# Five small changes to the start, the joint and the end of an attention and convolution kernel

## The chip, the cores and the metric

One NeuronCore of one Trainium2 chip. The metric is the device time of one execution in microseconds (us), the median of several. Lower is better.

## The reference

Sixteen images of 128 channels and 32 x 32 pixels pass an attention block, then a block of two quantized 3x3 convolutions.

```
# attention: 4 heads, 1024 tokens of 128 channels
qkv    = einsum('bchw,oc->bohw', x, w_qkv) + b_qkv
attn   = softmax(q @ k * c**-0.5)
x      = einsum('bchw,oc->bohw', attn @ v, w_out) + b_out + x
# convolutions: activations to 4 bits, weights to 4 bits; batch normalization with the statistics
# of the whole batch (16 x 32 x 32 values of each channel)
out = batchnorm(conv3x3(act_quant(x),   weight_quant(w1)), gamma1, beta1)
out = batchnorm(conv3x3(act_quant(out), weight_quant(w2)), gamma2, beta2)
return out + x
```

The batch statistics are what matters: no value of the second convolution's input is known before the last matmul of the first convolution, and no output before the last matmul of the second.

## The kernel before

`wvo_sb` holds the value and output weights; they are multiplied into one matrix on TensorE (`fold_b`, tile `ps_b`) before any value can be projected. The start (cut):

```python
nc.sync.dma_start(out=wqk_sb[0 : P // 2, 0], in_=wqk[0 : P // 2, 0])
nc.scalar.dma_start(out=wqk_sb[P // 2 :, 0], in_=wqk[P // 2 :, 0])
nc.sync.dma_start(out=xt[0][:, ts(0, HALF)], in_=x[0][:, ts(0, HALF)])
nc.scalar.dma_start(out=xt[0][:, ts(1, HALF)], in_=x[0][:, ts(1, HALF)])
nc.scalar.dma_start(out=wvo_sb, in_=wvo)
nc.sync.dma_start(out=wqk_sb[:, 1:], in_=wqk[:, 1:])
load(1)
# ...
warm_up(3)
fold_a(0)
for hf in range(NHF):
    project_u(0, hf)
fold_b()
# ... then, step by step: scores(g, j), project_v, attend one step later
```

The attention body in the middle (some 2030 us) is untouched. One piece of convolution, with its copy out of PSUM (the memory that the matmuls of this kernel write to) and, for the last image alone, its statistics straight from PSUM:

```python
def conv(pool, tag, b, n, r, rows=RPH, group=None):
    ps = pool.tile([P, rows, W], F32, tag=tag, name=f"psc{n}_{b}_{r}")
    for tap in range(NTAP):
        ...                                     # nine matmuls, bf16
    ps = ps.rearrange("p h w -> p (h w)")
    nc.scalar.copy(ys[b][:, r * W : (r + rows) * W], ps)
    if group is not None:
        nc.vector.bn_stats(place(n, b, group), ps)
    return last
```

The tiles for the statistics stand in memory just ahead of the output tiles:

```python
early = [keep.tile([P, (B - LATE) * NHF, STATS], F32, name=f"early{n}") for n in range(2)]
late = [
    keep.tile([P, 3 + (LATE * NHF + 1 - n) * STATS], F32, name=f"late{n}") for n in range(2)
]
# ...
ys = [keep.tile([P, N], F32, name=f"y{b}") for b in range(B)]
```

Between the convolutions `keep_clock` issues 21 matmuls whose result nobody reads, so that TensorE does not stand idle. Then the second convolution and the output (B is 16 images, H 32 rows, RPH 16 rows, NHF 2 halves of an image, N 1024 values of a row of a tile):

```python
for r0, r1 in ((0, RPH + 1), (RPH + 1, H)):       # 17 and 15 rows of 32
    quantize(0, ys[0], scale1, bias1, r0, r1)      # ScalarE, then two steps on VectorE
quantize(1, ys[1], scale1, bias1)
for b in range(B):
    for hf in range(NHF):
        conv(ps_c, "c", b, 1, hf * RPH, group=hf if b == B - 1 else None)
    ...
scale2, bias2 = bn_params(1)
for b in range(B):
    parts = NHF if b == 0 else 1
    for i in range(parts):
        cut = ts(i, N // parts)
        y = ys[b][:, cut]
        nc.scalar.activation(y, y, AF.Identity, bias=bias2, scale=scale2)
        nc.vector.tensor_tensor(y, y, x1[b][:, cut], ALU.add)
        nc.sync.dma_start(out=out[b][:, cut], in_=y)
```

## Time and profile before

| | us |
|---|---|
| time, median of 3 runs | 2154.43 (2154.38 to 2155.27) |
| time of the one execution that was profiled | 2156.01 |
| its span | 2154.1 |
| TensorE busy | 2118.2 (98%) |
| first matmul that needs the value weights | 10.13 |
| end of the last matmul of convolution 1, start of the first of convolution 2 | 2054.18, 2059.34 |
| end of the last matmul of convolution 2, end of the bias of its normalization | 2122.99, 2126.33 |

The chain of work that ended last is read from its end backwards: each line is a stretch of time and what the next line waited for. A line of DMA, of ACT (ScalarE) or of DVE (VectorE) in it, between lines of PE (TensorE), is time in which TensorE had nothing that it could start, or filled with matmuls that nobody reads. The prediction shows the lines of the start and of both joints.

The page's view by stretches shows the stores. Its columns are: the stretch, its length, busy us and number of instructions of PE, PEld, DVE, ACT and POOL, the granted TensorE clock, the share of the DMA engines, and GB/s. The kernel before, while the first stores go out:

```profile
2129.00:2130.00 1.00, 0.00 (x0) 0.00 (x0) 0.96 (x1) 1.00 (x2) 0.00 (x0) 0.50 0.99 383
2130.00:2131.00 1.00, 0.00 (x0) 0.00 (x0) 1.00 (x2) 1.00 (x2) 0.00 (x0) 0.50 0.15 55
2131.00:2132.00 1.00, 0.00 (x0) 0.00 (x0) 1.00 (x2) 1.00 (x2) 0.00 (x0) 0.50 0.92 381
```

Image 0 goes out by 2130, then the DMA stands still for most of a microsecond until image 1 is ready; from there on it is never idle.

### The profile page before, as it was taken

To read this page: it belongs to the slowest core of one execution; us is meant where nothing else is said; L and a number is where in the kernel's file an instruction comes from. 1 tells how busy PE (TensorE), PEld (TensorE's weight loads), DVE (VectorE), ACT (ScalarE), POOL (GpSimd) and SP (SyncE) were. 2 spreads that over 40 slices of the span, in tenths; PEclk is the share of its full clock that TensorE was granted. 3 is DMA by queue.
4 is the path that set the end of the run, shared out by engine and by line. 5 is a ranking of instruction groups with operands and counts; after the bars stand their busy time and mean duration, and the time that the engine had idled before them with its cause. 6 is when DMAs were issued, how large, how long until landed. Compare 5 with 4: busy or idle time off the path is not lost.

```text
span 2154.1 us, 14436 instructions
## 1 busy us (share of the span) xinstructions
PE 2118.2 (98%) x5293; PEld 947.3 (44%) x5294; DVE 1256.5 (58%) x1791; ACT 695.3 (32%) x764; POOL 6.8 (0%) x16
## 2 busy tenths in 40 slices
PE   9999999999999999999999999999999999999994
PEld 4444444444444444444444444444444444444541
DVE  3665565556456565556646555665655655665676
ACT  2233232333233333333323323333332333323355
POOL 0000000000000000000000000000000000000000
PEclk9999999999999999999999999999999999999997
DMA  1000000000000000000000000000000000000043
GB/s 60 11 20 0 0 20 0 20 0 10 10 0 20 0 20 0 0 20 0 20 0 20 0 0 20 0 20 0 18 3 0 20 0 10 1 0 10 0 166 157
DMA packets 10606, 36.79 MB, mean 17 GB/s; under 512 B 1440, under 2 KB 1568, under 8 KB 10528
## 3 DMA queue, kind: packets, MB, share of 16 engines
q1 hardware_dynamic: 9872, 33.76, 4.2%
q10 hardware_dynamic: 656, 2.03, 0.3%
q8 instruction: 43, 0.70, 0.1%
q14 instruction: 35, 0.29, 0.0%
HBM read 19.01 MB, written 16.78 MB: 17 GB/s over the span
## 4 chain that ended last, share of the span: by engine, by line
PE 98%; DVE 1%; DMA 0%; ACT 0%; issue 0%; ACTq 0%; DVEq 0%
PE pss L480 41%; PE psa L504 40%; PE psc L275 6%; PE psv L459 5%; PE psu L448 5%; PE psa L619 1%; DVE y L777 1%; DMA wvo_sb<-in_wvo_dram 0%; ACT y L776 0%; DVE late L285 0%; PE ps_b L420 0%; ACT y L283 0%; DVEq L963 0%; PE ps_a L412 0%; ACTq L386 0%
## 5 line engine op out<-in xcount | busy, mean ns | idle before, releaser
L480 PE MATMUL pss<-u,x 128*128 128x512 f32 (+1 forms) x2064 | 962.4, 589 | 0.0
L504 PE MATMUL psa<-e,vo 128*128 128x512 f32 x2016 | 947.6, 592 | 0.0
L493 ACT ACTIVATE e<-pss 128x1024 f32<-128x1024 f32 x511 | 522.9, 1023 | 1305.3 <-PE pss L480 1269.2
L515 DVE TENSOR_TENSOR es<-es,e 128x1024 f32<-128x1024 f32 x378 | 461.3, 1220 | 475.3 <-ACT e L493 471.5
L480 PEld LDWEIGHTS pss<-u,x 128*128 128x128 f32 x2064 | 392.1, 190 | 487.2 <-issue 467.8
L504 PEld LDWEIGHTS psa<-e,vo 128*128 128x128 f32 x2016 | 382.6, 190 | 471.4 <-issue 466.4
L467 DVE COPY vo<-psv 128x512 f32<-128x512 f32 x128 | 88.2, 689 | 259.7 <-PE psv L459 259.7
L275 PE MATMUL psc<-pad,wq 128*128 128x512 bf16 (+3 forms) x585 | 132.0, 380 | 0.6 <-DVE pad L250 0.6
L448 PE MATMUL psu<-x,at_sb 128*128 128x512 f32 x256 | 131.1, 594 | 0.2 <-DVE at_sb L414 0.2
L459 PE MATMUL psv<-bt_sb,x 128*128 128x512 f32 x256 | 130.4, 592 | 0.0
L453 DVE TENSOR_SCALAR u<-psu,au_sb 128x512 f32<-128x512 f32 x64 | 47.9, 749 | 87.2 <-PE psu L448 87.2
L275 PEld LDWEIGHTS <-wq 128*128 128x128 bf16 x585 | 56.7, 97 | 79.9 <-issue 15.3
L527 DVE TRANSPOSE_TENSOR_REDUCE part<-es 128x32 f32<-128x1024 f32 (+1 forms) x66 | 80.6, 1221 | 2.2
L562 DVE STREAM_TRANSPOSE rb<-sums 128x1024 f32<-128x1024 f32 (+1 forms) x66 | 80.1, 1213 | 2.3
L513 DVE TENSOR_TENSOR es<-e,e 128x1024 f32<-128x1024 f32 x63 | 76.6, 1216 | 0.0
L448 PEld LDWEIGHTS psu<-x,at_sb 128*128 128x128 f32 x256 | 48.8, 191 | 61.3 <-issue 60.5
L459 PEld LDWEIGHTS psv<-bt_sb,x 128*128 128x128 f32 x256 | 48.6, 190 | 61.2 <-issue 61.2
L573 DVE TENSOR_TENSOR av<-av,rb 128x1024 f32<-128x1024 f32 x47 | 57.6, 1226 | 3.3
L574 DVE TENSOR_TENSOR acc<-acc,av 128x1024 f32<-128x1024 f32 x47 | 57.4, 1221 | 1.0
L283 ACT COPY y<-psc 128x512 f32<-128x512 f32 (+2 forms) x65 | 37.5, 578 | 59.2 <-PE psc L275 58.7
L520 ACT COPY av<-psa 128x512 f32<-128x512 f32 x63 | 36.9, 586 | 44.6 <-PE psa L504 44.6
L553 DVE COPY side<-part 32x32 f32<-32x32 f32 x252 | 43.0, 171 | 4.7
(98 smaller groups left out, 467.2 us busy)
## 6 DMA issues: line engine op xcount, KB each, us to landing
x_dram<-x SPq DMA_DIRECT2D x16, 512.0 KB, 2.6
res<-x_dram SPq DMA_DIRECT2D x16, 512.0 KB, 9.9
x<-in_x_dram SPq DMA_DIRECT2D x15, 512.0 KB, 3.6
out_dram<-y SPq DMA_DIRECT2D x15, 512.0 KB, 4.7
raw<-in_cw_dram ACTq DMA_DIRECT2D x2, 576.0 KB, 3.7
wvo_sb<-in_wvo_dram ACTq DMA_DIRECT2D x1, 514.0 KB, 7.8
out_dram<-y SPq DMA_DIRECT2D x2, 256.0 KB, 2.0
wqk_sb<-in_wqk_dram SPq DMA_DIRECT2D x1, 385.5 KB, 7.0
```

Of the source, the lines that this page charges most:

```text
L275: last = nc.tensor.matmul(ps, lhsT=wq[n][:, tap, :], rhs=pads[b % NPAD][:, r + dy : r + dy + rows, dx : dx + W], start=(tap == 0), stop=(t ...
L448: nc.tensor.matmul(ps, lhsT=at_sb[:, h, :], rhs=xt[b][:, ts(hf, HALF)], start=True, stop=True)
L459: nc.tensor.matmul(ps, lhsT=xt[b][:, ts(j, P)], rhs=bt_sb.rearrange("p h o -> p (h o)"), start=True, stop=True,)
L467: nc.vector.tensor_copy(vos[b, j], ps)
L480: last = nc.tensor.matmul(ps[:, ts(m, N // len(parts))], lhsT=xt[b][:, ts(key, P)], rhs=us[g][:, queries], start=True, stop=True,)
L493: exps[:] = [nc.scalar.activation(e, ps, AF.Exp).ins]
L504: nc.tensor.matmul(psa[g][m], lhsT=vos[b, j][:, ts(h, P)], rhs=e[:, ts(m, HALF)], start=(j == 0), stop=(j == NCH - 1),)
L513: nc.vector.tensor_tensor(es[g], es.pop((g, 0)), es.pop((g, 1)), ALU.add)
L515: added = nc.vector.tensor_tensor(es[g], es[g], es.pop((g, j)), ALU.add)
L527: nc.vector.tensor_reduce(part, total.rearrange("p (k c) -> p k c", c=Q), AX.X, ALU.add, apply_transpose=True,)
L562: nc.vector.transpose(rb, rinv.unsqueeze(2).to_broadcast([P, n, Q]))
L573: nc.vector.tensor_tensor(av, av, rb, ALU.mult)
```

## The change

Its intent: let the value weights land earlier, take the copy out of the chain ahead of the statistics, begin and end the second convolution with pieces of 8 rows so that the quantization ahead of it and the statistics behind it are short, and begin storing earlier.

```diff
@@ -227,7 +227,7 @@
     STATS = nc.vector.BN_STATS_DIM
     early = [keep.tile([P, (B - LATE) * NHF, STATS], F32, name=f"early{n}") for n in range(2)]
     late = [
-        keep.tile([P, 3 + (LATE * NHF + 1 - n) * STATS], F32, name=f"late{n}") for n in range(2)
+        keep.tile([P, 3 + (LATE * NHF + 1) * STATS], F32, name=f"late{n}") for n in range(2)
     ]
     for n in range(2):
         nc.gpsimd.memset(late[n][:, 0:1], float((B - LATE) * N))
@@ -280,9 +280,9 @@
                 stop=(tap == NTAP - 1),
             )
         ps = ps.rearrange("p h w -> p (h w)")
-        nc.scalar.copy(ys[b][:, r * W : (r + rows) * W], ps)
         if group is not None:
             nc.vector.bn_stats(place(n, b, group), ps)
+        nc.scalar.copy(ys[b][:, r * W : (r + rows) * W], ps)
         return last
 
     def statistics(b, n):
@@ -384,7 +384,8 @@
         nc.scalar.dma_start(out=wqk_sb[P // 2 :, 0], in_=wqk[P // 2 :, 0])
         nc.sync.dma_start(out=xt[0][:, ts(0, HALF)], in_=x[0][:, ts(0, HALF)])
         nc.scalar.dma_start(out=xt[0][:, ts(1, HALF)], in_=x[0][:, ts(1, HALF)])
-        nc.scalar.dma_start(out=wvo_sb, in_=wvo)
+        nc.sync.dma_start(out=wvo_sb[0 : P // 2], in_=wvo[0 : P // 2])
+        nc.scalar.dma_start(out=wvo_sb[P // 2 :], in_=wvo[P // 2 :])
         nc.sync.dma_start(out=wqk_sb[:, 1:], in_=wqk[:, 1:])
         load(1)
         nc.sync.dma_start(out=bo_sb, in_=bo)
@@ -666,7 +667,7 @@
             ps = ps_a.tile([P, HALF], F32, tag="a0", name="unread")
             flat = wq[0].rearrange("p t o -> p (t o)")
             with tc.issue_after(convs[0]):
-                for _ in range(21):
+                for _ in range(16):
                     nc.tensor.matmul(
                         ps, lhsT=wq[1][:, 0, :], rhs=flat[:, 0:HALF], start=True, stop=True
                     )
@@ -751,12 +752,15 @@
             t = resp.tile([P, N], F32, name=f"res{b}")
             nc.sync.dma_start(out=t, in_=x1d[b])
             x1.append(t)
-        for r0, r1 in ((0, RPH + 1), (RPH + 1, H)):
+
+        for r0, r1 in ((0, 10), (10, RPH + 2), (RPH + 2, H)):
             quantize(0, ys[0], scale1, bias1, r0, r1)
         quantize(1, ys[1], scale1, bias1)
+        starts = {0: (0, 8, RPH, H), B - 1: (0, RPH, H - 8, H)}
         for b in range(B):
-            for hf in range(NHF):
-                conv(ps_c, "c", b, 1, hf * RPH, group=hf if b == B - 1 else None)
+            rows = starts.get(b, (0, RPH, H))
+            for i, (r0, r1) in enumerate(zip(rows, rows[1:])):
+                conv(ps_c, "c", b, 1, r0, r1 - r0, group=i if b == B - 1 else None)
             if b + 2 < B:
                 quantize(b + 2, ys[b + 2], scale1, bias1)
             if b < B - 1:
@@ -769,13 +773,15 @@
         scale2, bias2 = bn_params(1)
 
         for b in range(B):
-            parts = NHF if b == 0 else 1
-            for i in range(parts):
-                cut = ts(i, N // parts)
-                y = ys[b][:, cut]
-                nc.scalar.activation(y, y, AF.Identity, bias=bias2, scale=scale2)
-                nc.vector.tensor_tensor(y, y, x1[b][:, cut], ALU.add)
-                nc.sync.dma_start(out=out[b][:, cut], in_=y)
+            ends = (0, N // 4, N // 2, N) if b == 0 else (0, N)
+            for lo, hi in zip(ends, ends[1:]):
+                y = ys[b][:, lo:hi]
+                if (b, lo) == (0, 0):
+                    nc.vector.tensor_scalar(y, y, scale2, bias2, ALU.mult, ALU.add)
+                else:
+                    nc.scalar.activation(y, y, AF.Identity, bias=bias2, scale=scale2)
+                nc.vector.tensor_tensor(y, y, x1[b][:, lo:hi], ALU.add)
+                nc.sync.dma_start(out=out[b][:, lo:hi], in_=y)
     outer.close()
 
 
```

## The prediction

> **What bounds the kernel now.** I read the page's busy times first, then the chain of work that ended last over the whole span, then the same chain and the order of time at the start (0 to 30 us) and at the end (2028 us on), and last the stretches of the DMA.
>
> From the page: TensorE is the bound nearly everywhere.
>
> ```profile
> PE 2118.2 (98%) x5293; PEld 947.3 (44%) x5294; DVE 1256.5 (58%) x1791; ACT 695.3 (32%) x764; POOL 6.8 (0%) x16
> ```
>
> 98% of 2154.1 us leaves 36 us in which TensorE does not work. Nothing in the change touches the attention body, so all that can be won lies in those 36 us: the start, the joint between the two convolutions, and the output. Chain of work at the start (start us, length us, what):
>
> ```profile
> 2.22 7.77 DMA wvo_sb<-in_wvo_dram
> 9.99 0.14 issue
> 10.13 1.13 PE ps_b L420 x8
> ```
>
> The value weights land at 9.99, TensorE waits for them (its own wait there is 2.85 us, 7.28 to 10.13), and everything after is continuous on TensorE; so an earlier landing moves all the rest. The chain at the end:
>
> ```profile
> 2048.07 6.11 PE psc L275 x36
> 2054.18 0.02 issue
> 2054.20 0.41 ACT y L283
> 2054.61 0.02 issue
> 2054.63 0.48 DVE late L285
> ...
> 2057.21 0.85 ACT qt L248
> 2058.06 0.02 issue
> 2058.08 0.45 DVE qt L249
> 2058.53 0.02 issue
> 2058.56 0.73 DVE pad L250
> 2059.29 0.05 issue
> 2059.34 63.66 PE psc L275 x288
> 2122.99 0.02 issue
> 2123.02 0.59 ACT y L283
> 2123.61 0.02 issue
> 2123.63 0.71 DVE late L285
> ...
> 2126.36 3.79 ACT y L776 x4
> ```
>
> So each convolution ends in copy, then statistics, then eight tiny instructions, and only then do quantization and the next convolution (or the output) begin. After 2126.36 the output pass is limited by the stores: in the stretches after it the DMA moves 86, 383 and 55 GB/s in the three microseconds from 2128, then 381 and from 2132 on about 410 GB/s until 2150. There is a hole at 2130 to 2131, and after it the stores never run dry.
>
> [...] the statistics, which only read the same PSUM tile as the copy, start 0.02 us after the copy ends. [...] The trace has 0.724 us for 544 columns written as 17 rows, 0.430 for 512 as 16 rows, 0.658 for 480 as 15 rows[...] In the trace the idle 2.85 us at the start cost nothing (granted clock 1.00), so the shorter holes after the change should not either.
>
> **The change part by part**, in us against the time before.
>
> A. Value weights. Ahead of wvo or beside it now go wqk of head 0 (0.13 MB), x of image 0 (0.52 MB), wqk of the other heads (0.39 MB) and, alternating, part of x of image 1. The DMA packets of wvo start at 5.73, most engines are through at 7.8, one straggling engine ends at 9.38, and 0.6 later it counts as landed. After the change half of wvo goes where wqk of the other heads went, the other half runs beside those. About 0.4 to 0.6 MB less moves before wvo is complete; at the 330 to 410 GB/s of these stretches that is 1.0 to 1.8. The landing should come at 8.2 to 9.0, still after the 7.28 at which TensorE becomes free, so all of it counts. **-1.5.** The other heads' wqk came at 8.97 and is first read at 16.25; 1 to 2 us later does no harm.
>
> B. Statistics ahead of the copy, end of convolution 1. The statistics (0.48) start after the matmuls instead of after the 0.41 copy: -0.43. But the copy (0.40) now sits in ScalarE's queue ahead of the square root, which is ready 0.02 + 0.30 after the statistics: +0.05. And the order of instructions on VectorE moves around 2045: the statistics of the piece of 480 columns (0.63) and a quantization step (0.27, which itself waits for ScalarE until about 2045.55) now stand ahead of the transposing reduction of the last softmax sums. In the trace before:
>
> ```profile
> 2044.99 0.70 DVE L527 TRANSPOSE_TENSOR_REDUCE part<-es 128x16 f32<-128x512 f32 x1
> 2045.62 0.63 DVE L285 BATCH_NORM_STATS2 late<-psc 128x6 f32<-128x480 f32 x1
> 2046.16 0.51 PE L545 MATMUL psr<-part,quad 128*128 128x8 f32 x4
> ```
>
> The reduction ended at 2045.69, TensorE read it at 2046.16. Worked anew: statistics 2044.99 to 2045.62, step to 2045.82, reduction 2045.75 to 2046.45, so TensorE's psr can start at 2046.50, 0.34 later, with everything behind it: +0.34. Sum of B: **-0.04**; the gain is nearly lost.
>
> C. Quantization before convolution 2, from bias to first matmul. Was 0.85 + 0.45 + 0.73 (544 columns, 17 rows). For 10 rows: ScalarE 0.85 less 224 columns at 0.83 ns = 0.66; first VectorE step between 0.28 (256) and 0.44 (544): 0.31; second step[...] between 0.30 (256) and 0.43 (512): 0.33. 1.30 against 2.03: **-0.73**. Do the later chunks come in time? From the bias: the second chunk is padded at about 2.0, wanted at 2.45; the third, which waits for one of two buffers, at 3.0, wanted at 3.5; image 1 at 4.8, wanted at 5.4. Thin, but enough. The 16 filler matmuls (0.22 each, 3.5) end inside the hole of now 4.0; 21 of them (4.6) would have blocked the convolution, so their cut belongs to the gain.
>
> D. Splits at both ends of convolution 2. 18 matmuls more, at half width. The last 18 pieces of convolution 1, of 256 and 288 columns, took 0.12 each (6.11 less 18 x 0.22, over 18), against 0.22 for 512: two halves cost about 0.003 to 0.006 more each. **+0.10.**
>
> E. End of convolution 2. Copy 0.59 and two issue steps gone, statistics of 256 columns (0.43, as the 256-column piece of convolution 1) for 512 (0.71): -0.90; the copy ahead of the square root +0.05, a slightly longer aggregation +0.02. **-0.83.**
>
> F. First stores. The first store is issued about 0.8 after the bias instead of 1.6. But the hole in the DMA before image 1 stays, because that store waits for ScalarE's 1024 columns and VectorE's addition. ScalarE did 512, 512, 1024 before image 1 was ready; now 256 goes to VectorE and it does 256, 512, 1024. One 256-column step of ScalarE is 0.21. The stores of images 1 to 15 then run at 410 GB/s as before. **-0.21**, not -0.8.
>
> Sum: -1.5 - 0.04 - 0.73 + 0.10 - 0.83 - 0.21 = -3.2, so 2154.43 - 3.2 = 2151.2 us.
>
> **Rivals.** R1: wvo is limited by the straggling engine, not by its place in the queue. For it: one engine ended 1.6 after most others. Then A is -0.8 and the time 2151.9. If, on the contrary, the landing falls to 7.3, A is -2.8 (TensorE's own work until 7.28 stops it there) and the time 2149.9. R2: the VectorE reordering does not stall TensorE (the reduction has some slack that I put too low), or stalls it more: 2150.9 or 2151.6. R3: a wait takes the place of the shortened quantization: the third chunk or image 1 comes late and TensorE stands at 2062; for it, thin slack of 0.4 to 0.6; against it, VectorE's writes with even rows are faster. It would give back up to 0.7: 2151.9. R4: the earlier first store is worth its full 0.8, if the store engines' total were the limit from the first byte; against it the hole in the DMA at 2130. Then 2150.6. R5: with fewer filler matmuls the clock falls for convolution 2. Against it the 2.85 us hole at the start with a granted clock of 1.00. [...]
>
> **Range and chances.** The terms' errors (A 0.5, B 0.3, C to F 0.3 together) and about 0.5 of spread between runs (the three runs span 0.9) make some 0.9 as one standard deviation at most, so 2149.6 to 2152.9. The whole change is 0.15% of the time; 2% would be 43 us, more than all of TensorE's idle time. So within 2% is all but certain.
>
> **What would show it.** A: wvo lands at 8.2 to 9.0 and TensorE's ps_b follows at once. B: the statistics wait for TensorE, not ScalarE; a stall of 0.3 to 0.4 ahead of psr, with the reduction as the releaser. C: 1.4 to 1.5 from bias to first matmul, one hole of about 0.5 behind the filler matmuls. D: the convolution takes 63.75 from first to last matmul. E: some 2.5 from last matmul to bias, against 3.34. F: a hole in the DMA still ahead of image 1's store. The prediction is wrong if TensorE waits inside convolution 2, if the clock falls below 1.00 there, or if wvo lands as late as before.

## The result

| | before | changed |
|---|---|---|
| time, median of 6 runs, us | 2154.41 (2154.34 to 2155.27) | 2153.41 (2152.61 to 2155.77) |
| span of the profiled execution | 2154.1 | 2151.1 |
| its time | 2156.01 | 2153.01 |

The ratio is 0.9995, with a 95% interval of 0.9982 to 1.0008. A ratio here is the mean time of one kernel's fast runs over that of the other's of the same rounds, so not quite the ratio of the medians. The predicted range was 2149.6 to 2152.9; the median lies 0.5 us above it.

The two profiles differ by 3.0 us, nearly the 3.2 that was predicted, and the medians by 1.0. The prediction was right about one pair of executions, by luck as the runs below show (a late landing before, an ordinary one after), and wrong about the kernels. The page of the changed kernel:

```profile
PE 2117.1 (98%) x5306; PEld 948.0 (44%) x5307; DVE 1256.9 (58%) x1796; ACT 696.1 (32%) x767; POOL 6.9 (0%) x16
```

Its chain at the start:

```profile
2.22 6.61 DMA wvo_sb<-in_wvo_dram
...
8.92 1.13 PE ps_b L421 x8
```

And at the joint and the end (L284 is now the statistics, L285 the copy):

```profile
2053.26 0.48 DVE late L284
...
2053.76 0.35 ACT y L285
...
2054.16 0.40 ACT rt L314
...
2055.84 0.66 ACT qt L248
...
2056.52 0.34 DVE qt L249
...
2056.88 0.34 DVE pad L250
...
2057.27 63.70 PE psc L275 x306
...
2120.99 0.44 DVE late L284
...
2123.48 4.71 ACT y L782 x5
```

The copy has left its place ahead of the statistics and stands, as predicted, ahead of the square root `rt`. From the end of the last matmul (2053.23) to the first of convolution 2 (2057.27) the joint is now 4.04 us instead of 5.16. The stall in front of `psr` is there too (`psr` are the matmuls that read `part`, the softmax sums that VectorE has just reduced). In the order of time (start us, length us, instruction, and in brackets the idle time before it and what ended it):

```profile
2043.58 0.66 DVE L284 BATCH_NORM_STATS2 late<-psc 128x6 f32<-128x480 f32 x1
...
2044.35 0.71 DVE L528 TRANSPOSE_TENSOR_REDUCE part<-es 128x16 f32<-128x512 f32 x1
...
2045.11 0.52 PEld L546 LDWEIGHTS psr<-part,quad 128*128 128x128 f32 x4 [0.39 <-DVE part L528]
```

The reduction now follows the statistics, and TensorE stands for 0.39 us until it is done.

### The profile page after: what moved, and what is told of

It reads as the page before. It is cut to its first block, busy times and chain, and to the rows that moved or that the text cites. A ratio compares the mean times of both kernels' runs of the same rounds, so it can differ in the third digit from the quotient of the medians.

```text
span 2151.1 us, 14475 instructions
## 1 busy us (share of the span) xinstructions
PE 2117.1 (98%) x5306; PEld 948.0 (44%) x5307; DVE 1256.9 (58%) x1796; ACT 696.1 (32%) x767; POOL 6.9 (0%) x16
## 4 chain that ended last, share of the span: by engine, by line
PE 98%; DVE 1%; ACT 0%; DMA 0%; issue 0%; ACTq 0%; DVEq 0%
PE pss L481 41%; PE psa L505 40%; PE psc L275 6%; PE psv L460 5%; PE psu L449 5%; PE psa L620 1%; DVE y L783 1%; DMA wvo_sb<-in_wvo_dram 0%; ACT y L782 0%; PE ps_b L421 0%; DVEq L969 0%; PE psr L546 0%; DVE late L284 0%; PE ps_a L413 0%; ACTq L386 0%
## 5 line engine op out<-in xcount | busy, mean ns | idle before, releaser
L285 ACT COPY y<-psc 128x512 f32<-128x512 f32 (+3 forms) x67 | 37.9, 565 | 59.1 <-PE psc L275 53.8
```

## The experiments

Since most of TensorE's work is a fixed chain, two executions can be compared by a few marks. The first four columns of this table are read from the traces (us); the last is the time, the median of five runs (one run where marked), with that of the kernel before of the same call in brackets. "Body" is from the start of `ps_b` to the start of the last matmul of convolution 1, "conv 2" from its first matmul to its end, "end" from there to the first store packet of image 1, "stores" from that packet to the end of the last one.

| run | ps_b starts | body | end | stores | time (before) |
|---|---|---|---|---|---|
| before, first profile | 10.13 | 2043.75 | 8.15 | 20.42 | |
| changed, first profile | 8.92 | 2044.01 | 7.09 | 20.95 | |
| b_again | 8.68 | 2043.75 | 8.15 | 20.22 | 2154.70 (2155.43) |
| a_only | 8.81 | 2043.75 | 8.15 | 20.60 | 2154.57 (2155.43) |
| no_a | 9.02 | 2044.21 | 7.07 | 20.93 | 2153.35 (2155.43) |
| no_stall | 8.36 | 2043.75 | 7.08 | 20.96 | 2152.24 (2155.43) |
| b_shift | 9.99 | 2043.75 | 8.15 | 20.64 | 2155.28 (2155.12) |
| align | 9.41 | 2043.75 | 7.08 | 20.30 | 2152.48 (2155.12) |
| late_b | 8.34 | 2043.12 | 7.08 | 20.69 | 2151.39 (2155.12) |
| a_again | 8.62 | 2044.11 | 7.08 | 20.98 | 2153.39 (2155.12) |
| b_again2 | 9.10 | 2043.75 | 8.15 | 20.36 | 2154.97 (2154.67) |
| a_only2 | 9.46 | 2043.76 | 8.15 | 20.55 | 2154.79 (2154.67) |
| b_shift64 | 8.98 | 2043.75 | 8.14 | 20.62 | 2154.95, one run (2154.67) |
| b_shift128 | 9.15 | 2043.75 | 8.14 | 20.65 | 2155.15, one run (2154.67) |

Convolution 2 took 63.64 us in every run with its old pieces and 63.69 in every run with the new ones. All runs gave the correct result. The kernel before, in three calls of nine runs, had medians of 2155.43, 2155.12 and 2154.67, and single runs from 2154.13 to 2157.25: a difference of half a microsecond between two medians of five proves nothing, and where it matters the marks decide. The experiments ran on three chips. Of all these ratios only that of no_stall has an interval that leaves out 1 (0.9984, 0.9970 to 0.9998), and all are within 2%.

### b_again: the kernel before, unchanged

> The kernel before, unchanged, to see how one execution differs from another. Theory 1 (the profile that the prediction read was of a slow execution: its time was 2156.0 against a median of 2154.4, and the excess sits in the start): the value weights land at about 8.4 instead of 9.99, TensorE's ps_b starts at about 8.5, the span is about 2152.5, and time minus span stays 1.9. Theory 2 (the start was typical, the excess sits in the output): wvo lands at 9.9 to 10.1 again and the stretch from the last bias (2126.3) to the end of the span is 26 us instead of 27.8. Theory 3 (noise of the chip's clock): the stretch from ps_b to the end of convolution 1, 2044.05 us on TensorE, is longer or shorter by 1 us or more. Time against before: same, within 0.3 us, in all three.

The profiled execution took 2154.22 us. Chain at the start:

```profile
2.22 6.33 DMA wvo_sb<-in_wvo_dram
...
8.68 1.13 PE ps_b L420 x8
```

The same kernel starts `ps_b` 1.45 us earlier than in its first profile, by the landing alone. The body is equal to 0.01 us, so is everything up to the stores, and the time less the span is 1.9. That is theory 1, for 1.45 of the 1.79 us between the two executions; the rest lies behind the first store of image 1. The first profile shows a late landing: its last packet of `wvo` ended at 9.38, here at 8.04. In time the expectation (within 0.3 us of before) failed: 2154.70 against 2155.43, for one and the same kernel.

### a_only: the split of the value weights alone, on the kernel before

```diff
-        nc.scalar.dma_start(out=wvo_sb, in_=wvo)
+        nc.sync.dma_start(out=wvo_sb[0 : P // 2], in_=wvo[0 : P // 2])
+        nc.scalar.dma_start(out=wvo_sb[P // 2 :], in_=wvo[P // 2 :])
```

> Only the split of the value weights. Theory 1: the landing is within 0.5 of that of the kernel before of the same call (8.3 to 8.9), and the time within 0.5 us of before. Theory 2: the landing is 1.1 to 1.5 earlier than that of before, and so is the time: -1.2 us.

2154.57 us against 2154.70 for b_again. That is 0.86 below the kernel before of the call, more than the 0.5 of theory 1, but b_again, which is that kernel, was 0.73 below it too. `ps_b` is not earlier (8.81 against 8.68). Theory 2 falls.

### no_a: the changed kernel without that split

> The changed kernel with the value weights loaded by one transfer, as before. Theory 1: as fast as the changed kernel, -1.0 to -1.6 us against before, since the other parts are worth 1.7 us by the two profiles. Theory 2: the other parts give less than that in the unprofiled runs; the time is within 0.5 us of before.

2153.35 us, against 2153.41 and 2153.39 of the changed kernel: what the change gains, it gains without its first part. The median is 2.1 below the kernel before of this call, more than expected; but that kernel's median was high here by 0.7 (it is the same kernel as b_again).

### no_stall: the old order for one piece

```diff
+        copy_first = (n, r) == (0, 0)
+        if copy_first:
+            nc.scalar.copy(ys[b][:, r * W : (r + rows) * W], ps)
         if group is not None:
             nc.vector.bn_stats(place(n, b, group), ps)
-        nc.scalar.copy(ys[b][:, r * W : (r + rows) * W], ps)
+        if not copy_first:
+            nc.scalar.copy(ys[b][:, r * W : (r + rows) * W], ps)
```

> The changed kernel, but the copy of the first piece (480 columns) of the last image of convolution 1 stays ahead of its statistics, so that VectorE's order there is that of before. Both theories: no idle time of TensorE ahead of psr (0.39 us in the changed kernel's profile), TensorE's chain from ps_b to the last matmul of convolution 1 is 0.25 to 0.4 us shorter than 2044.31, and the time 0.3 us below the changed kernel's.

```profile
2043.01 0.70 DVE L532 TRANSPOSE_TENSOR_REDUCE part<-es 128x16 f32<-128x512 f32 x1
...
2043.63 0.63 DVE L287 BATCH_NORM_STATS2 late<-psc 128x6 f32<-128x480 f32 x1
2044.18 0.63 PEld L550 LDWEIGHTS psr<-part,quad 128*128 128x128 f32 x4
```

The reduction is first again, and TensorE does not wait. The body is 2043.75 as before the change; in the changed kernel it was 2044.01, 2044.11 and (no_a) 2044.21. So the stall costs 0.26 to 0.46 us, and it comes from the order of two instructions on VectorE. The time fell by 1.1 us, more than the stall accounts for (0.3 was expected). In the profiled run the rest is the start, which was early (`ps_b` at 8.36); in the other four no trace shows it. None of the five was 2 us above the others, as one of six and two of five of the changed kernel's were.

### b_shift, b_shift64, b_shift128: where the output tiles start

In every run of the changed kernel the stores took some 20.95 us, and in the kernel before 20.2 to 20.6. The prediction had taken them as equal. In the trace the single store packets (4096 bytes, one row of a tile) were longer, 163.6 ns in the mean against 159.7. The diff has one line that nobody would take for a change in speed: `late1` grew from 27 to 33 values, for the added statistics. In the built programs it takes 32 bytes more for that, and all sixteen tiles `y` behind it start 32 bytes past a multiple of 256 instead of on one: `y0` stands at byte 32256 of each partition before, at 32288 in the changed kernel and in b_shift, at 32512 in align. So I moved them in the kernel before, with whatever stands behind them, and changed nothing else:

```diff
+    keep.tile([P, 8], F32, name="shift")     # 32 bytes; 16 and 32 values in the other two
     ys = [keep.tile([P, N], F32, name=f"y{b}") for b in range(B)]
```

> The kernel before with an unused tile of 32 bytes ahead of the output tiles y, so that each row of them starts 32 bytes past a multiple of 256, as in the changed kernel; nothing else. Theory (the store packets are slower from such addresses): mean packet time of the 1920 stores of images 1 to 15 goes from 159.7 ns to 163.6, the stretch from their first to their last packet from 20.2-20.6 us to 20.9, the time +0.4 to +0.5 us. Rival (the slower stores come from the 256-column first stores, or from VectorE's new work beside them): packets stay at 159.7 ns and the time at that of before.

> The kernel before with 64 unused bytes ahead of y, so rows start 64 bytes past a multiple of 256. If any start off a multiple of 256 costs the same, the mean store packet takes 163 to 164 ns; if a start on a multiple of 64 is enough, 159.7 ns.

> The same with 128 bytes. 163 to 164 ns if only multiples of 256 are fast, 159.7 ns if multiples of 64 or 128 are enough.

Mean length of the 1920 packets that store images 1 to 15, computed from the packets in each trace:

| tiles y start at | runs | ns |
|---|---|---|
| a multiple of 256 bytes | before, b_again, b_again2, a_only, a_only2, align, late_b | 159.6 to 159.8 |
| 32 past it | changed, a_again, no_a, no_stall, b_shift | 163.5 to 163.6 |
| 64 past it | b_shift64 | 163.9 |
| 128 past it | b_shift128 | 164.2 |

The same in the stretches, 16 us in the midst of the stores; first the kernel before, then b_shift:

```profile
2132.00:2148.00 16.00, 0.00 (x0) 0.00 (x0) 14.16 (x13) 12.85 (x12) 0.00 (x0) 0.50 1.02 415
```

```profile
2132.00:2148.00 16.00, 0.00 (x0) 0.00 (x0) 14.03 (x13) 12.73 (x12) 0.00 (x0) 0.50 1.02 405
```

The engines are fully busy in both (share 1.02) and move 2.4% less in b_shift. The changed kernel itself:

```profile
2129.00:2145.00 16.00, 0.00 (x0) 0.00 (x0) 14.06 (x13) 12.76 (x12) 0.00 (x0) 0.50 1.02 406
```

So each of the three starts off 256 costs, by 2.4 to 2.8% a packet; by what mechanism, no run here shows.

While all 16 engines are at work the cost stands clear of any spread: from the first packet of image 1 until the number of packets in flight falls below 12 for good, counted in each trace, takes 18.83 to 18.91 us in the seven aligned runs and 19.42 to 19.46 in the other seven. In the last 1.2 to 1.9 us of every run mostly two packets or one are in flight, and that tail varies by itself. So the whole stretch "stores" shows less: 20.64 in b_shift (20.9 was expected) against 20.22 to 20.60 in the aligned runs of the old order. In time, b_shift was 0.16 above its kernel before and not 0.4: too little to be seen there. b_shift64 and b_shift128 settled their question: a start on a multiple of 64 or 128 is not enough (163.9 and 164.2 ns a packet).

### align: aligned tiles, no stall

no_stall with 224 unused bytes ahead of `y`, so that the tiles start on a multiple of 256 again:

```diff
+    keep.tile([P, 56], F32, name="shift")
     ys = [keep.tile([P, N], F32, name=f"y{b}") for b in range(B)]
```

> The changed kernel without the stall ahead of psr (as no_stall), and with 224 unused bytes ahead of y, so that its rows start at multiples of 256 bytes again. Theory: store packets back at 159.7 ns, the stretch from first to last of them at 20.2-20.6 us, time 0.3 to 0.5 us below no_stall, so -2.6 to -3.2 us against before on the same chip. Rival: packets stay at 163.6 ns, time as no_stall.

```profile
2130.00:2146.00 16.00, 0.00 (x0) 0.00 (x0) 13.29 (x12) 11.98 (x11) 0.00 (x0) 0.50 1.02 415
```

415 GB/s again, packets of 159.6 ns, "stores" 20.30 instead of 20.96. The expectation of the trace held. That of the time against no_stall (0.3 to 0.5 lower) did not: 2152.48 against 2152.24. They were run at other times. In the two profiled runs `ps_b` began 1.05 us later than no_stall's, which is more than the alignment gives; for the medians the cause stays open. Against before, -2.6 us by the medians, as expected; ratio 0.9987 (0.9973 to 1.0000).

### late_b: the fold of the value weights behind the first scores

As align, with:

```diff
         for hf in range(NHF):
             project_u(0, hf)
-        fold_b()
 ...
-                if g == 0:
-                    project_v(0, j)
+                if step == 0:
+                    fold_b()
+                elif g == 0:
+                    if j == 1:
+                        project_v(0, 0)
+                    project_v(0, j)
```

> As align, and the fold of the value weights (ps_b) is put behind the first half of the first scores on TensorE, which need no value weights; the first projections of values follow the second scores. Theory (with the landing of wvo at about 8.0 to 8.9 TensorE idles 0.4 to 1.4 us ahead of ps_b): the idle time is filled, and TensorE's start is 0.6 to 0.9 us earlier than in align; time -0.6 to -0.9 us against align. Rival (a new wait comes for it, on ScalarE's copy of the folded weights or on VectorE's order): within 0.3 us of align.

Order of time on TensorE:

```profile
7.25 1.02 PE L486 MATMUL pss<-u,x 128*128 128x512 f32 x2
8.34 1.16 PE L426 MATMUL ps_b<-wvo_sb 128*128 128x128 f32 x8
9.34 2.74 PE L486 MATMUL pss<-u,x 128*128 128x512 f32 x6
```

TensorE computes the first two of these matmuls, half of the first scores, while the weights land. The body is 0.63 us shorter (2043.12), as that work has gone ahead of `ps_b`. The median is 2151.39, 1.1 below align and 3.7 below the kernel before, the lowest of all; but two of the five executions took 2153.89 and 2154.89, so that the ratio is 0.9988 (0.9974 to 1.0002). The gain of 0.63 in the body is shown, in one profile; the median's lead over align is not shown to be more than chance.

### a_again, b_again2, a_only2: repetitions

> The changed kernel once more, unchanged, to see how its executions differ. Everything from ps_b to the stores within 0.3 us of the first profile (stall ahead of psr 0.2 to 0.5; 63.69 us of convolution 2; 7.1 from its end to the first packet of image 1; store packets 163.6 ns); the landing of wvo, and with it ps_b, anywhere between 8.3 and 9.9. Time -0.7 to -1.6 us against before.

> The kernel before, unchanged, a second time, on the same chip and in the same rounds as a_only2: what the start is worth in a typical execution. Landing of wvo between 8.0 and 9.4, ps_b between 8.6 and 10.1, all else to 0.1 us as in the first profile; time as before.

> Only the split of the value weights, a second time. Theory 1 (the typical landing of the kernel before is already early): median 0 to 0.6 us below b_again2. Theory 2 (the split is worth what the first profile says): 1.1 to 1.5 below.

a_again repeats the first profile of the changed kernel in all marks (table). Its time was 2153.39, 1.7 below the kernel before of its call (0.7 to 1.6 was expected). Its start differs in one thing: `ps_b` began at 8.62 instead of 8.92. b_again2 and a_only2 ran on the same chip in the same rounds: 2154.97 and 2154.79. The chain of a_only2's start shows how little the split decides:

```profile
2.23 7.14 DMA wvo_sb<-in_wvo_dram
...
9.46 1.13 PE ps_b L421 x8
```

Over all profiles, `ps_b` began at 8.68, 8.98, 9.02, 9.10, 9.15, 9.99 and 10.13 with one transfer, and at 8.36, 8.62, 8.81, 8.92, 9.41 and 9.46 with two (late_b left out): medians 9.10 and 8.87. The split is worth 0.2 us or so, within a spread of more than one, and neither kind is always ahead on one chip (b_again 8.68 and no_a 9.02 against a_only 8.81 and no_stall 8.36; b_again2 9.10 against a_only2 9.46).

The packets show why it is so little. The last packet of `wvo` ends earlier with two transfers, at 7.97 in the median against 8.45. But the weights count as landed 0.7 to 1.2 us after that packet with two transfers, and 0.5 to 0.6 after it with one. About half of the gain is lost there; why, no run here shows. In the two late profiles, before and b_shift, the last three of the 128 packets of `wvo` end one by one, 0.31 us apart (in before at 8.76, 9.07 and 9.38), as from one engine; that is the one that R1 calls straggling.

## Why the prediction was wrong

**The step that failed first is A**, "-1.5". Its working started from a landing at 9.99, read from one execution, and counted the bytes that would no longer be ahead. In that execution the landing was late. Of the six other profiles with one transfer, five show `ps_b` between 8.68 and 9.15, and one (b_shift) at 9.99. The forecast landing, 8.2 to 9.0, came (8.83), but an unchanged kernel lands there too (8.55 in b_again, 8.96 in b_again2): the prediction's own sign of being wrong, "if wvo lands as late as before", is what happened, to within 0.2 us. What the split can take away was therefore about 0.2 us by the traces and 0.1 to 0.2 by the times (a_only and a_only2 against b_again and b_again2), not 1.5. The warning was in the numbers on hand: that execution's time of 2156.01 lay 1.6 above the median. A profile that is slower than the median must not give a difference that is then taken from the median. R1 named the straggling engine, which was in the right direction, but its -0.8 was still too much. By the medians of five, the split into partition halves gave -0.13 and -0.18 us. Two smaller readings of A were off: 7.28 is no fixed time at which TensorE becomes free (in the other profiles the first `psu` matmuls ended from 7.28 to 8.82), and the other heads' wqk is first read by a weight load at 15.82, not at 16.25.

**The second is a sentence of F**, that the stores of images 1 to 15 "then run at 410 GB/s as before". They ran at 406 where the kernel before had 415, since a statistics tile grew and moved the output tiles off their alignment; by the means of "stores", 20.45 for seven aligned runs and 20.89 for the five at 32 past, +0.44 us. (These two groups touch, with late_b at 20.69 and b_shift at 20.64. In the old order the shift alone gave 0.2, in the new one the way back from no_stall to align gave 0.66.)

With A at -0.2 and +0.44 for the stores, the predicted sum of -3.2 becomes -1.5. The measured differences of medians are -1.0 (6 runs each) and -1.7 (a_again). The rest, up to half a microsecond, is within what the kernel before itself shows. One more term stood in no account: from the end of the last store packet to the end of the span the old order takes 2.18 to 2.70 us and the new one 2.12 to 2.21, by the traces. That is another 0.3 in the change's favour in the medians of these stretches; its cause was not looked for.

The other steps held, each by the marks:

- **B.** Statistics straight after the matmul, copy ahead of the square root: predicted -0.43 + 0.05 from the last matmul to the square root; measured 0.93 (2053.23 to 2054.16) against 1.35 (2054.18 to 2055.53), -0.42. The queueing behind the copy cost only 0.02 of the 0.05: the root started 0.10 after its input was there, against 0.08. The stall of +0.34 was found at 0.26 to 0.46.
- **C.** From bias to first matmul predicted 1.30 plus issue, -0.73; measured 2055.81 to 2057.27, 1.46 against 2.16: -0.70. VectorE's step of 10 rows took 0.33 as interpolated, that of 14 rows 0.40. No chunk came late: convolution 2 ran through (TensorE busy for 63.65 of the 63.70 us from 2057.30 on), so R3 fell.
- **D.** Predicted +0.10; 63.69 against 63.64: +0.05.
- **E.** From last matmul to bias predicted -0.83; measured 2.48 against 3.34: -0.86.
- **F**, its own term. From the bias to the first packet of image 1, 4.60 against 4.80: -0.20, predicted -0.21. The hole in the DMA stayed, so R4 fell. One line of the changed kernel's stretches shows it:

```profile
2127.00:2128.00 1.00, 0.00 (x0) 0.00 (x0) 1.00 (x2) 1.00 (x2) 0.00 (x0) 0.50 0.06 23
```

- **R5** fell: with 16 filler matmuls TensorE idled 0.59 us ahead of convolution 2 (0.64 before), whose granted clock stayed at 1.00.

**What stays open.** Some executions of several kernels take 1.8 to 3.5 us more than their median (changed: 2155.77, 2156.23; no_a: 2155.58; late_b: 2154.89; before: 2157.25, 2156.74). None of them was profiled; a late landing could explain 1 to 1.4 us of it, as in the first profile of before and that of b_shift (2156.01 both), but not all. Why one DMA engine lags at the start, and which, the traces do not tell.

## What to carry to other kernels

Compare the profiled execution's own time with the median before reading a gain of a microsecond from it, and take a landing at the start from several executions: here the last packet of the same 0.5 MB ended between 8.04 and 9.38 us in three profiles of one unchanged program. A statistics tile that grows by a few values can move every tile behind it, here all sixteen output tiles by 32 bytes; look at the addresses of what the DMA streams. Here stores of 4096-byte rows on multiples of 256 bytes took 159.6 to 159.8 ns a packet, and 163.5 to 164.2 at 32, 64 and 128 bytes past one; at 32 past they moved 405 GB/s instead of 415. When two instructions change places on an engine that is not the bound, look at what stood behind them: here 0.3 to 0.5 us of the gain was lost to a reduction that TensorE was waiting for.
